# GpSimd's bias additions in two halves: cross-attention and a factored feed-forward layer on one core

## The chip, the core and the metric

The kernel runs on one core of a Trainium2 chip. The core has engines that run side by side, each with its own instruction queue: TensorE (PE, matmuls; its weight loads are listed apart as PEld), VectorE (DVE), ScalarE (ACT), GpSimd (POOL) and SyncE (SP, which here issues most of the DMAs). They meet through semaphores. The on-chip memory is SBUF; matmul results land in PSUM. The metric is the device time of one execution in microseconds (us), as the median of a few runs.

## The reference

The input x has 8 batches of 1024 rows of 1024 float32 numbers. What is computed:

```python
def _layernorm(x, axis=-1, eps=1e-05):
    m = jnp.mean(x, axis=axis, keepdims=True)
    v = jnp.var(x, axis=axis, keepdims=True)
    return (x - m) / jnp.sqrt(v + eps)
...
def reference(x, ctx_2048, mask_BxS2_bk0, L0_ffn_factors, L0_ffn_bias):
    def _L0_xattn_ref(hidden_states, memory_tokens, memory_mask):
        ...
        scores = jnp.einsum('bsd,bmd->bsm', hidden_states, memory_tokens) * scale
        scores = jnp.where(memory_mask[:, None, :], scores, neg_inf)
        attn = jax.nn.softmax(scores, axis=-1)
        readout = jnp.einsum('bsm,bmd->bsd', attn, memory_tokens)
        ...
    def _L0_ffn_ref(x, factors, bias):
        ...
        mixed = jnp.einsum('btd,rde->bte', x, factors)
        mixed = mixed / math.sqrt(rank) + bias
        return mixed
    x = x + _L0_xattn_ref(_layernorm(x, axis=-1), ctx_2048, mask_BxS2_bk0)
    x = x + _L0_ffn_ref(_layernorm(x, axis=-1), L0_ffn_factors, L0_ffn_bias)
    return x
```

The memory has 64 tokens in each batch, and there are 8 factors of 1024x1024. So each row attends to 64 tokens, the readout is added to it, the sum is normalized, multiplied by the sum of the factors, scaled, and added back together with the bias.

## The kernel before

The 8192 rows are worked in 16 groups of 512 rows. A group holds four row tiles of 128x1024 in SBUF, the tiles x. A tile is found by two numbers, h and q, as tile 2h+q. The steps of a group are: load the rows (load_rows, and once more in another layout, load_blocks); transpose them on VectorE (transpose_blocks, line 356, two instructions of 128x256 a call); scores on TensorE (line 399) with softmax (lines 426 to 439: line 426 reads PSUM, line 431 adds the mask in SBUF); the readout (line 465) and its addition to x (residual, line 473); the statistics and the normalization (normalize, line 534, ScalarE, which reads the tile x and writes h); a DMA that turns h into another layout (relayout), and VectorE's transposes of it (line 560); then the product with the summed factors.

That product is done by Strassen's scheme: seven products of half-size blocks, three of which (2, 3 and 4) are again split in seven. The operands' sums are formed by VectorE in combine_rows (lines 573 to 582, 128x512) and combine_parts (lines 621 to 631, 128x256): each of these instructions reads two SBUF tiles. TensorE multiplies in product (line 592) and part (line 641). VectorE adds each result, scaled, to x in give (line 605, 128x512) and give_part (line 655, 128x256): these read PSUM and the tile x.

The bias is added to x as a separate step, add_bias (line 540), between the normalization of a tile and the last addition of its products. It runs on GpSimd, on a whole tile of 128x1024, and reads two SBUF tiles, x and the broadcast bias. One tile of the first group has it on VectorE (add_bias_v, line 544). GpSimd has little else: small instructions on 128x2 numbers for the means and the reciprocal deviations (lines 317 to 346 and 490 to 520), on the way to the normalization.

The order is written out by hand. Two tables of step names, START and LOOP, are run line by line under a manual schedule; each engine takes its instructions in this order. START prepares the factors (their sum, and the combined blocks for the split products, combine_factors, lines 728 to 731) together with the first group and parts of the next. LOOP is run once for each group g, with p the group before it, n the next and m the one after that. In one pass it adds the bias of the tiles 3 and 1 of g and of the tiles 0 and 2 of n. PSUM banks and SBUF tiles are handed out from lists of free ones.

Of the kernel before, what the change touches and what calls it, by code (L numbers as in the profile page):

```python
# [10 lines left out]
F32 = mybir.dt.float32  # L11
BF16 = mybir.dt.bfloat16
AF = mybir.ActivationFunctionType
ALU = mybir.AluOpType
# [20 lines left out]
normalize 0 0 1; load_factor 1 7; load_factor 2 3; load_factor 2 5; load_factor 1 4;  # L35
transpose_h_pe 0 0 0; sum_factor 2 7; add_factor 1 7; load_factor 1 3; transpose_x_pe 1 0;
load_factor 1 6; add_sums 0 0; transpose_h_pe 0 0 1; read_out 0 1 0; add_factor 2 3;
add_bias 0 0 1; sum_factor 2 5; load_rows 1 3; load_factor 1 1; residual 0 1 0; norm_stats 0 1 0;
sum_factor 1 4; sum_factor 1 1; load_factor 2 1; load_rows 1 2; combine_rows 0 0 1;
sum_factor 2 1; norm_stats 0 1 1; add_factor 1 3; load_factor 2 2; add_factor 1 6;  # L40
load_factor 2 0; add_sums 1 1; row_sums 1 0; load_factor 3 0; add_sums 1 0; transpose_x_pe 1 1;
add_factor 2 2; add_factor 2 0; add_bias_v 0 0 0; add_sums 2 1; row_squares 1 0; load_factor 3 4;
add_factor 3 4; scores 1; add_factor 3 0; add_sums 2 0; product 0 0 1; load_factor 3 2;
normalize 0 1 0; normalize 0 1 1; transpose_h_pe 0 1 0; load_factor 3 3; add_factor 3 3;
row_sums 1 1; load_factor 3 1; load_factor 3 6; combine_rows 0 0 2; load_factor 3 7;
transpose_h_pe 0 1 1; product 0 0 5; row_squares 1 1; combine_rows 0 0 3; load_factor 3 5;
add_factor 3 2; sum_factor 3 1; combine_rows 0 0 4; scores_back 1; sum_factor 3 6; give 0 0 1;
load_rows 2 1; load_rows 2 0; add_factor 3 7; combine_rows 0 1 1; sum_factor 3 5; softmax 1;
add_sums 3 1; row_sums 2 0; product 0 1 1; weights_back 1; product 0 0 6; add_sums 3 0;
read_out 1 0 0; combine_parts 0 4 1; combine_factors 4; residual 1 0 0; read_out 1 0 1;  # L50
combine_rows 0 1 2; part 0 4 2; give 0 0 6; part 0 4 1; give_part 0 4 1; combine_parts 0 4 2;
combine_rows 0 1 3; part 0 4 5; residual 1 0 1; load_blocks 2 1; load_blocks 2 0;
combine_rows 0 1 4; product 0 0 7; give 0 1 1; norm_stats 1 0 0; row_squares 2 0;
give_part 0 4 2; combine_parts 0 4 3; read_out 1 1 0; add_bias 0 1 0; norm_stats 1 0 1;
product 0 1 6; part 0 4 6; combine_parts 0 2 1; load_rows 2 2; residual 1 1 0; read_out 1 1 1;
combine_parts 0 4 4; give_part 0 4 6; give 0 1 6; residual 1 1 1; product 0 1 5; normalize 1 0 0;
product 0 1 7; give_part 0 4 5; combine_factors 3; normalize 1 0 1; load_memory 2;
combine_factors 2; part 0 4 7; give 0 0 5; give_part 0 4 7; give 0 0 7; part 0 4 3; part 0 2 1;
transpose_blocks 2 0 0; part 0 2 5; norm_sums 1 1; centre_memory 2; transpose_blocks 2 0 1;
give_part 0 4 3; combine_parts 0 2 2; give_part 0 2 1; transpose_blocks 2 0 2; part 0 4 4;  # L60
combine_parts 0 3 1; transpose_memory 2; relayout 1 0; give_part 0 4 4; part 0 3 1; part 0 3 2;
add_bias 1 0 0; transpose_blocks 2 1 0; store 0 2; part 0 2 6; give_part 0 3 2; part 0 3 5;
transpose_blocks 2 1 1; give_part 0 2 5; norm_squares 1 1; transpose_blocks 2 0 3;
transpose_blocks 2 1 2; part 0 2 2; normalize 1 1 0; combine_parts 0 2 3; transpose_blocks 2 1 3;
normalize 1 1 1; give_part 0 2 6; combine_parts 0 2 4; combine_parts 0 3 2; transpose_rows 1 0 0;
# [2 lines left out]
product 1 0 1; give_part 0 3 5; scores_back 2; relayout 1 1; part 0 3 6; combine_rows 1 0 2;  # L68
give_part 0 2 7; give_part 0 3 6; product 1 0 5; combine_parts 0 3 4; give 0 1 7; part 0 3 3;
part 0 3 7; softmax 2; give_part 0 2 3; give 1 0 1; combine_rows 1 0 3; part 0 2 4;  # L70
transpose_rows 1 1 0; product 1 0 6; give_part 0 3 7; add_bias 0 1 1; weights_back 2; part 0 3 4;
store 0 3; give_part 0 2 4; read_out 2 0 0; read_out 2 0 1; add_bias 1 0 1; transpose_rows 1 1 1;
add_bias 1 1 0; give 1 0 6; give_part 0 3 4; product 1 1 1;
"""

LOOP = """
# [1 line left out]
product g 0 6; give p 1 5; transpose_rows g 1 0; give_part p 3 4; give g 0 5; give_part p 2 3;  # L78
give g 0 6; weights_back n; transpose_rows g 1 1; part p 3 3; read_out n 0 0; give_part p 3 2;
combine_rows g 1 1; read_out n 0 1; residual n 0 0; residual n 0 1; give_part p 3 3;  # L80
product g 1 1; combine_parts g 4 1; product g 0 7; load_blocks m 1; add_bias g 1 1;
combine_rows g 0 4; read_out n 1 0; norm_stats n 0 0; combine_rows g 1 2; read_out n 1 1;
norm_stats n 0 1; transpose_blocks m 0 0; part g 4 5; end_rows p 1; end_rows p 0; part g 4 1;
residual n 1 0; product g 1 5; store p 3; combine_rows g 1 3; combine_parts g 4 2;
give_part g 4 1; part g 4 6; combine_rows g 1 4; give g 1 1; product g 1 6; normalize n 0 0;
combine_parts g 2 1; normalize n 0 1; add_bias n 0 0; store p 1; transpose_blocks m 0 1;
give_part g 4 5; part g 2 5; combine_parts g 4 3; load_memory m; give_part g 4 6;
combine_parts g 4 4; residual n 1 1; combine_parts g 2 2; store p 0; part g 2 1; give g 0 7;
part g 4 7; give g 1 6; combine_parts g 3 1; norm_sums n 1; part g 4 2; centre_memory m;
part g 3 1; part g 4 3; combine_parts g 2 3; give_part g 4 7; give_part g 4 2; add_bias g 1 0;  # L90
give_part g 2 1; transpose_memory m; transpose_blocks m 0 2; norm_squares n 1;
combine_parts g 2 4; part g 4 4; give_part g 3 1; give_part g 2 5; give_part g 4 4;
transpose_blocks m 0 3; part g 2 6; give_part g 2 6; add_bias n 0 1; give_part g 4 3;
combine_parts g 3 2; part g 3 5; relayout n 0; product g 1 7; load_rows m 0; normalize n 1 0;
transpose_blocks m 1 0; transpose_blocks m 1 1; part g 3 6; combine_parts g 3 3; store g 2;
normalize n 1 1; part g 2 7; transpose_rows n 0 0; give g 1 7; load_rows m 2;
combine_parts g 3 4; give_part g 3 6; give_part g 2 7; transpose_rows n 0 1; load_rows m 1;
part g 2 2; load_rows m 3; transpose_blocks m 1 2; row_sums m 0; row_sums m 1;
transpose_blocks m 1 3; scores m; product n 0 1; scores_back m; combine_rows n 0 1; part g 3 7;
combine_rows n 0 2; row_squares m 0; give_part g 2 2; combine_rows n 0 3; give_part g 3 5;  # L100
part g 2 4; give_part g 3 7; product n 0 5; part g 3 4; relayout n 1;
# [4 lines left out]
def kernel(  # L106
# [17 lines left out]
    nc = tc.nc  # L124
    P = 128
# [7 lines left out]
    KH = NC // 2  # L133
    NS = NC // 2
    H = D // 2
    HH = H // 2
# [3 lines left out]
    ISR = 1.0 / math.sqrt(R)  # L140
# [8 lines left out]
    work = ctx.enter_context(tc.tile_pool(name="work", bufs=1))  # L149
# [3 lines left out]
    class Slots:  # L153
# [28 lines left out]
    bias_bc = const.tile([P, D], F32, name="bias_bc")  # L182
# [9 lines left out]
    SECOND = (2, 3, 4)  # L192
    PRODUCTS = {
        1: ("a11", "b11", "u", True, ((0, 0),)),
        5: ("s1", "t1", "v", True, ((1, 1), (0, 1)) if 3 in SECOND else ((1, 1),)),
        6: ("s2", "t2", "u", False, ((0, 1),)),
        3: ("s4", "b22", "v", False, ((0, 1),)),
        7: ("s3", "t3", "u", False, ((1, 1), (1, 0)) if 4 in SECOND else ((1, 1),)),
        2: ("a12", "b21", "z", True, ((0, 0),)),
        4: ("a22", "t4", "u", False, ((1, 0),)),  # L200
    }
    LAST = {"u": 7 if 4 in SECOND else 4, "v": 5 if 3 in SECOND else 3, "z": 2}
    PARTS = {
        1: ("a11", "u", True, (0, 0)),
        5: ("s1", "v", True, (1, 1)),
# [18 lines left out]
    st = {}  # L224
# [310 lines left out]
                to, fr, AF.Identity, bias=nb[:, h : h + 1], scale=rstd[:, h : h + 1]  # L535
            )

    def add_bias(g: int, q: int, h: int):
        xt = st["x", g, 2 * h + q]
        nc.gpsimd.tensor_add(xt, xt, bias_bc)  # L540

    def add_bias_v(g: int, q: int, h: int):
        xt = st["x", g, 2 * h + q]
        nc.vector.tensor_add(xt, xt, bias_bc)

    def relayout(g: int, q: int):
        h2 = st["h", g, q]
# [19 lines left out]
    def combine_rows(g: int, q: int, k: int):  # L567


        ops = st["ops", g, q]  # L570
        if k == 1:
            ops["s1"] = work.tile([P, KH, P], F32, tag="s1", name=f"s1_{g}_{q}")
            nc.vector.tensor_add(ops["s1"], ops["a21"], ops["a22"])
        if k == 2:
            ops["s2"] = work.tile([P, KH, P], F32, tag="s2", name=f"s2_{g}_{q}")
            nc.vector.tensor_sub(ops["s2"], ops["s1"], ops["a11"])
        if k == 3:
            nc.vector.tensor_sub(ops["a21"], ops["a11"], ops["a21"])
            ops["s3"] = ops["a21"]
        if k == 4:  # L580
            assert "s3" in ops
            nc.vector.tensor_sub(ops["a11"], ops["a12"], ops["s2"])
            ops["s4"] = ops["a11"]
# [17 lines left out]
    def give(g: int, q: int, p: int):  # L601
        key = PRODUCTS[p][2]
        for h, n in PRODUCTS[p][4]:
            xt = st["x", g, 2 * h + q][:, ts(n, H)]
            nc.vector.scalar_tensor_tensor(xt, st["y", g, q, key], ISR, xt, ALU.mult, ALU.add)  # L605
        if LAST[key] == p:
            banks.back(("y", g, q, key))
# [41 lines left out]

    def give_part(g: int, p: int, i: int):  # L650
        key = PARTS[i][1]
        h, n = PRODUCTS[p][4][0]
        q, k = PARTS[i][3]
        xt = st["x", g, 2 * h + q][:, 2 * n * HH + k * HH : 2 * n * HH + (k + 1) * HH]
        nc.vector.scalar_tensor_tensor(  # L655
            xt, st["yp", g, p, key][:, :HH], ISR, xt, ALU.mult, ALU.add
        )
        if LAST2[key] == i:
            banks.back(("yp", g, p, key))

# [125 lines left out]
```

## Time and profile before

| what | us |
|---|---|
| median of three runs | 981.09 (979.46 to 981.38) |
| the profiled execution | 981.39 |
| its span, first to last instruction | 979.6 |
| GpSimd's bias additions, 63 of 128x1024 | 150.1, mean 2.384 |
| VectorE line 627, 48 of 128x256, two SBUF inputs | 45.9, mean 0.957 |
| VectorE line 625, 48 of the same form | 20.9, mean 0.434 |
| VectorE line 582, 32 of 128x512, two SBUF inputs | 41.9, mean 1.308 |
| VectorE line 576, 32 of the same form | 21.4, mean 0.668 |
| VectorE line 431, 16 of 128x256, two SBUF inputs | 30.7, mean 1.916 |
| TensorE busy, 256 to 312 us | 55.04 of 56 |
| VectorE busy, 256 to 312 us | 50.20 of 56 |

The granted TensorE clock is 0.996 of full speed over the span. A profile of one execution gives each instruction's start and length. A group of instructions is one line, engine, operation and set of tiles; beside its busy time stands the idle time of its engine just before it, and what ended that. A chain of waits is followed back from a late instruction: at each step to what released it, or to the instruction before it on its engine. The last groups of the input differ from the steady loop, as do the first 200 us, in which the factors are loaded and summed.

### The profile page before, as it was taken

Reading aid. Unit: us, or ns where it says so; the run is one execution under the profiler, and the core shown is the slowest. Engines: PE = TensorE matmul, PEld = TensorE weight load, DVE = VectorE, ACT = ScalarE, POOL = GpSimd, SP = SyncE. Lnnn points to the kernel's source line nnn. Section 1 sums busy time; section 2 is a strip of 40 time slices with the busy share of each in tenths; the row PEclk is TensorE's granted clock in tenths of the full one; section 3 lists DMA queues with packets and bytes.
Section 4 is the critical chain, followed back from the end, with each engine's and each line's share of the span. In section 5 each row is a group of like instructions: output and inputs, shape, how many; then the busy total and the mean of one; then the engine's idle time right before and its main releaser. Section 6 shows DMA issues by size and latency. Waiting matters only on the chain.

```text
span 979.6 us, 11017 instructions
## 1 busy us (share of the span) xinstructions
PE 941.1 (96%) x3456; PEld 547.0 (56%) x3456; DVE 838.6 (86%) x1510; ACT 380.8 (39%) x712; POOL 237.9 (24%) x298
## 2 busy tenths in 40 slices
PE   3889999999999999999999999999999999999998
PEld 2345455655656565655656565564656565565656
DVE  3689999979799887989799697989889788989955
ACT  3035252443616253442623455351714445252300
POOL 0021124312312232411322142321223123132300
PEclk9999999999999999999999999999999999999999
DMA  9999637475565667366465756557474746542412
GB/s 353 418 421 369 179 107 159 126 177 145 158 156 155 151 194 149 109 168 165 153 162 155 164 144 148 140 162 176 151 177 134 172 123 170 142 151 79 100 70 86
DMA packets 93530, 167.01 MB, mean 170 GB/s; under 512 B 12320, under 2 KB 71840, under 8 KB 89376
## 3 DMA queue, kind: packets, MB, share of 16 engines
q1 hardware_dynamic: 93024, 165.20, 58.4%
q10 hardware_dynamic: 448, 1.11, 0.4%
q8 instruction: 27, 0.44, 0.2%
q14 instruction: 31, 0.25, 0.1%
HBM read 101.25 MB, written 33.55 MB: 138 GB/s over the span
## 4 chain that ended last, share of the span: by engine, by line
PE 60%; DVE 26%; DMA 5%; SPq 4%; issue 3%; ACT 1%; POOL 0%; DVEq 0%; ACTq 0%; POOLq 0%
PE yu L592 24%; PE yv L592 7%; PE ro L465 5%; PE y4u L641 4%; SPq L551 4%; PE y3u L641 4%; DVE xT L356 4%; DVE x L655 3%; DVE x L605 3%; DVE hT L560 3%; PE scT L399 3%; DMA f<-in_L_ffn_factors_dram 3%; DVE hT L627 3%; PE y2u L641 2%; PE y4v L641 2%
## 5 line engine op out<-in xcount | busy, mean ns | idle before, releaser
L534 ACT ACTIVATE h<-x,nb,rstd 128x512 f32<-128x512 f32 x128 | 96.2, 822 | 211.6 <-DVE x L473 134.2
L540 POOL TENSOR_TENSOR x<-x,bias_bc 128x1024 f32<-128x1024 f32 x63 | 150.1, 2384 | 73.5 <-DVE x L605 37.7
L592 PE MATMUL yu<-b,hT 128*128 128x512 f32 x256 | 118.0, 604 | 0.0
L592 PE MATMUL yu<-t,s 128*128 128x512 f32 x256 | 115.3, 593 | 0.1
L592 PE MATMUL yv<-t,s 128*128 128x512 f32 x256 | 115.2, 593 | 0.0
L592 PE MATMUL yu<-t,hT 128*128 128x512 f32 x256 | 115.1, 592 | 0.0
L605 DVE SCALAR_TENSOR_TENSOR x<-yu,x 128x512 f32<-128x512 f32 x128 | 82.9, 675 | 19.1 <-PE yu L592 19.1
L473 DVE SCALAR_TENSOR_TENSOR x<-ro,rden,x 128x512 f32<-128x512 f32 x128 | 88.4, 741 | 3.5 <-PE ro L465 3.5
L316 ACT ACTIVATE junk<-x 128x1024 bf16<-128x1024 f32 x60 | 63.2, 1054 | 56.6 <-DMA x<-in_x_dram 55.7
L356 DVE STREAM_TRANSPOSE xT<-xb 128x256 f32<-128x256 f32 x224 | 81.6, 410 | 0.0
L592 PEld LDWEIGHTS yu<-b,hT 128*128 128x128 f32 x256 | 46.3, 189 | 62.6 <-issue 51.8
L592 PEld LDWEIGHTS yu<-t,hT 128*128 128x128 f32 x256 | 48.6, 190 | 54.4 <-issue 50.5
L592 PEld LDWEIGHTS yu<-t,s 128*128 128x128 f32 x256 | 48.4, 190 | 48.7 <-issue 45.7
L592 PEld LDWEIGHTS yv<-t,s 128*128 128x128 f32 x256 | 48.5, 190 | 48.2 <-issue 45.9
L399 PE MATMUL scT<-xT,memT 128*64 128x256 f32 x512 | 66.5, 385 | 9.2 <-DVE xT L356 9.2
L560 DVE STREAM_TRANSPOSE hT<-hb 128x1024 f32<-128x1024 f32 x60 | 73.5, 1227 | 0.7 <-issue 0.6
L328 ACT ACTIVATE junk<-x,nmean 128x1024 bf16<-128x1024 f32 x60 | 68.9, 1149 | 2.9 <-POOL nmean L317 0.7
L490 POOL TENSOR_SCALAR rstd<-mv 128x2 f32<-128x2 f32 x17 | 4.6, 269 | 253.6 <-DVE mv L487 253.6
L465 PE MATMUL ro<-mem,eT 64*128 64x512 f32 x256 | 64.5, 617 | 0.6 <-ACT eT L454 0.6
L655 DVE SCALAR_TENSOR_TENSOR x<-y3u,x 128x256 f32<-128x256 f32 x64 | 26.2, 409 | 43.9 <-PE y3u L641 43.6
L502 ACT ACTIVATE junkz<-x 128x1024 bf16<-128x1024 f32 x30 | 31.7, 1056 | 72.7 <-DVE x L473 72.2
L399 PEld LDWEIGHTS scT<-xT,memT 128*64 128x64 f32 x512 | 37.3, 136 | 36.0 <-DVE xT L356 15.0
(133 smaller groups left out, 1544.2 us busy)
## 6 DMA issues: line engine op xcount, KB each, us to landing
f<-in_L_ffn_factors_dram SPq DMA_DIRECT2D x32, 1024.0 KB, 10.8
x<-in_x_dram SPq DMA_DIRECT2D x64, 512.0 KB, 4.5
out_dram<-x SPq DMA_DIRECT2D x64, 512.0 KB, 4.4
hb<-h SPq DMA_DIRECT2D x480, 64.0 KB, 2.0
xb<-in_x_dram SPq DMA_DIRECT2D x112, 256.0 KB, 6.9
mem<-in_ctx_dram SPq DMA_DIRECT2D x14, 256.0 KB, 3.8
mem<-in_ctx_dram ACTq DMA_DIRECT2D x2, 256.0 KB, 5.8
bias_bc<-in_L_ffn_bias_dram ACTq DMA_DIRECT2D x1, 512.0 KB, 7.9
```

The source lines that it names most:

```text
L316: nc.scalar.activation(junk, st["x", g, t], AF.Copy, accum_out=s1[:, t : t + 1])
L328: nc.scalar.activation(junk, st["x", g, t], AF.Square, bias=nmean[:, t : t + 1], accum_out=ss[:, t : t + 1])
L356: nc.vector.transpose(xT[:, 2 * e + c].rearrange("p (t j) -> p t j", j=Q), xb.rearrange("p t (k e i c) -> p e c t k i", e=NC // 2, i=2, c= ...
L399: nc.tensor.matmul(ps[ts(h, M), : 2 * P], mT[:, c, :], st["xT", g, h][:, c, :], start=(c == 0), stop=(c == NC - 1),)
L465: nc.tensor.matmul(ps, eT[ts(h, M), q, :], m[ts(h, M), ts(n, H)], start=True, stop=True)
L473: nc.vector.scalar_tensor_tensor(xt, st.pop(("ro", g, q, n, h)), rden[:, k : k + 1], xt, ALU.mult, ALU.add)
L534: nc.scalar.activation(to, fr, AF.Identity, bias=nb[:, h : h + 1], scale=rstd[:, h : h + 1])
L540: nc.gpsimd.tensor_add(xt, xt, bias_bc)
L560: nc.vector.transpose(st["hT", g, q][:, h].rearrange("p c (t j) -> p t c j", j=Q), hb[:, h].rearrange("p t (c i) -> p t c i", i=Q),)
L592: nc.tensor.matmul(ps, lhs[:, c, :], wq[right][:, c, :], start=(first and c == 0), stop=(c == KH - 1), skip_group_check=True,)
L605: nc.vector.scalar_tensor_tensor(xt, st["y", g, q, key], ISR, xt, ALU.mult, ALU.add)
L641: nc.tensor.matmul(ps, lhs[:, c, :], wp[p][i][:, c, :], start=(first and c == 0), stop=(c == 1), skip_group_check=True,)
```

## The change

Each call of add_bias now names a half tile: its last number k runs from 0 to 3, where k // 2 is the old h and k % 2 the half of 512 columns. In the tables each old entry is replaced by two, one behind the other at the same place. add_bias_v does the same on VectorE. So GpSimd has 126 additions of 128x512 in place of 63 of 128x1024, and VectorE two in place of one.

```diff
-add_bias 0 0 1; sum_factor 2 5; load_rows 1 3; load_factor 1 1; residual 0 1 0; norm_stats 0 1 0;
...
+add_bias 0 0 2; add_bias 0 0 3; sum_factor 2 5; load_rows 1 3; load_factor 1 1; residual 0 1 0;
...
-product g 1 1; combine_parts g 4 1; product g 0 7; load_blocks m 1; add_bias g 1 1;
...
+product g 1 1; combine_parts g 4 1; product g 0 7; load_blocks m 1; add_bias g 1 2;
+add_bias g 1 3; combine_rows g 0 4; read_out n 1 0; norm_stats n 0 0; combine_rows g 1 2;
...
-        6: ("s2", "t2", "u", False, ((0, 1),)),
+        6: ("s2", "t2", "u", False, ((0, 1), (1, 1), (1, 0)) if 7 in SECOND else ((0, 1),)),
...
-    LAST = {"u": 7 if 4 in SECOND else 4, "v": 5 if 3 in SECOND else 3, "z": 2}
+    LAST = {"u": 6 if 7 in SECOND else 7 if 4 in SECOND else 4, "v": 5 if 3 in SECOND else 3, "z": 2}
...
-    def add_bias(g: int, q: int, h: int):
-        xt = st["x", g, 2 * h + q]
-        nc.gpsimd.tensor_add(xt, xt, bias_bc)
-
-    def add_bias_v(g: int, q: int, h: int):
-        xt = st["x", g, 2 * h + q]
-        nc.vector.tensor_add(xt, xt, bias_bc)
+    def add_bias(g: int, q: int, k: int, eng=nc.gpsimd):
+
+        xt = st["x", g, 2 * (k // 2) + q][:, ts(k % 2, H)]
+        eng.tensor_add(xt, xt, bias_bc[:, ts(k % 2, H)])
+
+    def add_bias_v(g: int, q: int, k: int):
+        add_bias(g, q, k, nc.vector)
...
-            ops["s1"] = work.tile([P, KH, P], F32, tag="s1", name=f"s1_{g}_{q}")
+            ops["s1"] = work.tile([P, KH, P], F32, tag=f"s1{q if 5 in SECOND else ''}", name=f"s1_{g}_{q}")
...
-        h, n = PRODUCTS[p][4][0]
         q, k = PARTS[i][3]
-        xt = st["x", g, 2 * h + q][:, 2 * n * HH + k * HH : 2 * n * HH + (k + 1) * HH]
-        nc.vector.scalar_tensor_tensor(
-            xt, st["yp", g, p, key][:, :HH], ISR, xt, ALU.mult, ALU.add
-        )
+        for h, n in PRODUCTS[p][4]:
+            xt = st["x", g, 2 * h + q][:, ts(2 * n + k, HH)]
+            nc.vector.scalar_tensor_tensor(
+                xt, st["yp", g, p, key][:, :HH], ISR, xt, ALU.mult, ALU.add
+            )
```

SECOND is (2, 3, 4), at line 192, in both kernels.

More of the change, by code (lines that the diff above doesn't have):

```diff
@@ L37 @@
 load_factor 1 6; add_sums 0 0; transpose_h_pe 0 0 1; read_out 0 1 0; add_factor 2 3;
-add_bias 0 0 1; sum_factor 2 5; load_rows 1 3; load_factor 1 1; residual 0 1 0; norm_stats 0 1 0;
[L39 to L60, printed above, removed]
@@ L61 @@
-combine_parts 0 3 1; transpose_memory 2; relayout 1 0; give_part 0 4 4; part 0 3 1; part 0 3 2;
-add_bias 1 0 0; transpose_blocks 2 1 0; store 0 2; part 0 2 6; give_part 0 3 2; part 0 3 5;
+add_bias 0 0 2; add_bias 0 0 3; sum_factor 2 5; load_rows 1 3; load_factor 1 1; residual 0 1 0;
+norm_stats 0 1 0; sum_factor 1 4; sum_factor 1 1; load_factor 2 1; load_rows 1 2;
+combine_rows 0 0 1; sum_factor 2 1; norm_stats 0 1 1; add_factor 1 3; load_factor 2 2;
+add_factor 1 6; load_factor 2 0; add_sums 1 1; row_sums 1 0; load_factor 3 0; add_sums 1 0;
@@ new lines @@
+transpose_x_pe 1 1; add_factor 2 2; add_factor 2 0; add_bias_v 0 0 0; add_bias_v 0 0 1;
+add_sums 2 1; row_squares 1 0; load_factor 3 4; add_factor 3 4; scores 1; add_factor 3 0;
+add_sums 2 0; product 0 0 1; load_factor 3 2; normalize 0 1 0; normalize 0 1 1;
+transpose_h_pe 0 1 0; load_factor 3 3; add_factor 3 3; row_sums 1 1; load_factor 3 1;
+load_factor 3 6; combine_rows 0 0 2; load_factor 3 7; transpose_h_pe 0 1 1; product 0 0 5;
+row_squares 1 1; combine_rows 0 0 3; load_factor 3 5; add_factor 3 2; sum_factor 3 1;
@@ new lines @@
+combine_rows 0 0 4; scores_back 1; sum_factor 3 6; give 0 0 1; load_rows 2 1; load_rows 2 0;
+add_factor 3 7; combine_rows 0 1 1; sum_factor 3 5; softmax 1; add_sums 3 1; row_sums 2 0;
+product 0 1 1; weights_back 1; product 0 0 6; add_sums 3 0; read_out 1 0 0; combine_parts 0 4 1;
+combine_factors 4; residual 1 0 0; read_out 1 0 1; combine_rows 0 1 2; part 0 4 2; give 0 0 6;
+part 0 4 1; give_part 0 4 1; combine_parts 0 4 2; combine_rows 0 1 3; part 0 4 5; residual 1 0 1;
+load_blocks 2 1; load_blocks 2 0; combine_rows 0 1 4; product 0 0 7; give 0 1 1;
@@ new lines @@
+norm_stats 1 0 0; row_squares 2 0; give_part 0 4 2; combine_parts 0 4 3; read_out 1 1 0;
+add_bias 0 1 0; add_bias 0 1 1; norm_stats 1 0 1; product 0 1 6; part 0 4 6; combine_parts 0 2 1;
+load_rows 2 2; residual 1 1 0; read_out 1 1 1; combine_parts 0 4 4; give_part 0 4 6; give 0 1 6;
+residual 1 1 1; product 0 1 5; normalize 1 0 0; product 0 1 7; give_part 0 4 5;
+combine_factors 3; normalize 1 0 1; load_memory 2; combine_factors 2; part 0 4 7; give 0 0 5;
+give_part 0 4 7; give 0 0 7; part 0 4 3; part 0 2 1; transpose_blocks 2 0 0; part 0 2 5;
@@ L63 @@
+norm_sums 1 1; centre_memory 2; transpose_blocks 2 0 1; give_part 0 4 3; combine_parts 0 2 2;
+give_part 0 2 1; transpose_blocks 2 0 2; part 0 4 4; combine_parts 0 3 1; transpose_memory 2;
+relayout 1 0; give_part 0 4 4; part 0 3 1; part 0 3 2; add_bias 1 0 0; add_bias 1 0 1;
+transpose_blocks 2 1 0; store 0 2; part 0 2 6; give_part 0 3 2; part 0 3 5;
 transpose_blocks 2 1 1; give_part 0 2 5; norm_squares 1 1; transpose_blocks 2 0 3;
@@ L70 @@
 part 0 3 7; softmax 2; give_part 0 2 3; give 1 0 1; combine_rows 1 0 3; part 0 2 4;
-transpose_rows 1 1 0; product 1 0 6; give_part 0 3 7; add_bias 0 1 1; weights_back 2; part 0 3 4;
-store 0 3; give_part 0 2 4; read_out 2 0 0; read_out 2 0 1; add_bias 1 0 1; transpose_rows 1 1 1;
-add_bias 1 1 0; give 1 0 6; give_part 0 3 4; product 1 1 1;
+transpose_rows 1 1 0; product 1 0 6; give_part 0 3 7; add_bias 0 1 2; add_bias 0 1 3;
+weights_back 2; part 0 3 4; store 0 3; give_part 0 2 4; read_out 2 0 0; read_out 2 0 1;
+add_bias 1 0 2; add_bias 1 0 3; transpose_rows 1 1 1; add_bias 1 1 0; add_bias 1 1 1; give 1 0 6;
+give_part 0 3 4; product 1 1 1;
 """
@@ L80 @@
 combine_rows g 1 1; read_out n 0 1; residual n 0 0; residual n 0 1; give_part p 3 3;
-product g 1 1; combine_parts g 4 1; product g 0 7; load_blocks m 1; add_bias g 1 1;
-combine_rows g 0 4; read_out n 1 0; norm_stats n 0 0; combine_rows g 1 2; read_out n 1 1;
-norm_stats n 0 1; transpose_blocks m 0 0; part g 4 5; end_rows p 1; end_rows p 0; part g 4 1;
-residual n 1 0; product g 1 5; store p 3; combine_rows g 1 3; combine_parts g 4 2;
+product g 1 1; combine_parts g 4 1; product g 0 7; load_blocks m 1; add_bias g 1 2;
@@ L85 @@
+add_bias g 1 3; combine_rows g 0 4; read_out n 1 0; norm_stats n 0 0; combine_rows g 1 2;
+read_out n 1 1; norm_stats n 0 1; transpose_blocks m 0 0; part g 4 5; end_rows p 1; end_rows p 0;
+part g 4 1; residual n 1 0; product g 1 5; store p 3; combine_rows g 1 3; combine_parts g 4 2;
 give_part g 4 1; part g 4 6; combine_rows g 1 4; give g 1 1; product g 1 6; normalize n 0 0;
-combine_parts g 2 1; normalize n 0 1; add_bias n 0 0; store p 1; transpose_blocks m 0 1;
-give_part g 4 5; part g 2 5; combine_parts g 4 3; load_memory m; give_part g 4 6;
@@ L88 @@
[L88 to L98, printed above, removed]
+combine_parts g 2 1; normalize n 0 1; add_bias n 0 0; add_bias n 0 1; store p 1;
@@ new lines @@
+transpose_blocks m 0 1; give_part g 4 5; part g 2 5; combine_parts g 4 3; load_memory m;
+give_part g 4 6; combine_parts g 4 4; residual n 1 1; combine_parts g 2 2; store p 0; part g 2 1;
+give g 0 7; part g 4 7; give g 1 6; combine_parts g 3 1; norm_sums n 1; part g 4 2;
+centre_memory m; part g 3 1; part g 4 3; combine_parts g 2 3; give_part g 4 7; give_part g 4 2;
+add_bias g 1 0; add_bias g 1 1; give_part g 2 1; transpose_memory m; transpose_blocks m 0 2;
+norm_squares n 1; combine_parts g 2 4; part g 4 4; give_part g 3 1; give_part g 2 5;
@@ new lines @@
+give_part g 4 4; transpose_blocks m 0 3; part g 2 6; give_part g 2 6; add_bias n 0 2;
+add_bias n 0 3; give_part g 4 3; combine_parts g 3 2; part g 3 5; relayout n 0; product g 1 7;
+load_rows m 0; normalize n 1 0; transpose_blocks m 1 0; transpose_blocks m 1 1; part g 3 6;
+combine_parts g 3 3; store g 2; normalize n 1 1; part g 2 7; transpose_rows n 0 0; give g 1 7;
+load_rows m 2; combine_parts g 3 4; give_part g 3 6; give_part g 2 7; transpose_rows n 0 1;
+load_rows m 1; part g 2 2; load_rows m 3; transpose_blocks m 1 2; row_sums m 0; row_sums m 1;
```

## The prediction

> **What bounds the kernel now.** I read the page's busy times first, then the waits, then TensorE's timeline where it waits, then the chain backwards from there.
>
> ```profile
> PE 941.1 (96%) x3456; PEld 547.0 (56%) x3456; DVE 838.6 (86%) x1510; ACT 380.8 (39%) x712; POOL 237.9 (24%) x298
> ```
>
> TensorE (PE) bounds it; VectorE (DVE) is a close second; GpSimd (POOL), whose instructions change, is three quarters idle. So POOL's own time can't matter; whom it holds up can. The waits of PE between 200 and 872 us, the steady loop:
>
> ```profile
> PE scT L399 <- DVE xT L356: 8.4, 11, 0.8
> PE sc L417 <- ACT scTs L407: 0.5, 1, 0.5
> ```
>
> The loop has one recurring wait: the scores matmuls wait for VectorE's block transposes, once in each group (the whole trace has 12). PE ends are modelled, so I price it from starts. The timeline of PE at a scores block without the wait, then at one with it (start, length, both us):
>
> ```profile
> 199.05 3.67 PE L399 MATMUL scT<-xT,memT 128*64 128x256 f32 x32
> 202.65 0.70 PE L592 MATMUL yu<-b,hT 128*128 128x512 f32 x1
> ...
> 253.96 2.37 PE L399 MATMUL scT<-xT,memT 128*64 128x256 f32 x18
> 257.06 1.94 PE L399 MATMUL scT<-xT,memT 128*64 128x256 f32 x14 [0.73 <-DVE xT L356]
> 258.93 0.70 PE L592 MATMUL yu<-b,hT 128*128 128x512 f32 x1
> ```
>
> From the first scores matmul to the product behind it is 3.60 us undisturbed and 4.97 with the wait: 1.37 us lost. In the other parity of groups (309.40 to 314.44) it is 5.04, so 1.44. Twelve such waits, six of each parity, are 6 x 1.37 + 6 x 1.44 = **16.9 us**, all that can be won in the loop. Why are the transposes late? The chain of waits up to 257.06:
>
> ```profile
> 246.31 0.42 DVE x L655
> ...
> 249.72 2.49 DVE hT L627
> 252.20 1.16 DVE hT L560
> ...
> 257.06 1.94 PE scT L399 x14
> ```
>
> From 246.31, where VectorE last waited for PE, it works without a gap, and one instruction of it, L627, takes 2.5 us. The groups by line (min/median/max in ns) say what that should take:
>
> ```profile
> L627 DVE TENSOR_TENSOR hT<-hT,hT x48: 375/410/2584, 121.0 to 964.5; 128x256 f32<-128x256 f32 x48
> L582 DVE TENSOR_TENSOR hT<-hT,s x32: 681/686/2674, 98.4 to 949.2; 128x512 f32<-128x512 f32 x32
> L631 DVE TENSOR_TENSOR hT<-hT,r x48: 382/404/2533, 125.1 to 969.0; 128x256 f32<-128x256 f32 x48
> L431 DVE TENSOR_TENSOR sm<-sm,maskf x16: 424/2114/2342, 28.8 to 881.9; 128x256 f32<-128x256 f32 x16
> ```
>
> All four read two SBUF tiles. The stretched ones lie under a bias addition:
>
> ```profile
> 249.56 2.37 POOL L540 TENSOR_TENSOR x<-x,bias_bc 128x1024 f32<-128x1024 f32 x1
> 249.64 2.56 DVE L627 TENSOR_TENSOR hT<-hT,hT 128x256 f32<-128x256 f32 x1
> ```
>
> L627 ends at 252.20, 0.27 after the addition's end at 251.93. VectorE's operations with one SBUF input (L655 and L605 read PSUM and x; the transposes) keep their length under the same additions. The Trainium skill has this rule ("SBUF — State Buffer", Who interferes with whom): a VectorE instruction with two SBUF inputs and a GpSimd instruction that reads SBUF exclude each other for a whole instruction. The trace agrees, at about 2.2 us a hit.
>
> **The change, part by part.** *Work added.* 63 additions of 128x1024 become 126 of 128x512. The row of 128x1024 has 2.36 us (its median); the nearest row with hardly any elements, POOL's TENSOR_TENSOR at L493 (128x2), has 0.215. That gives (2.36 - 0.215) / 1022 = 2.1 ns an element and 0.215 + 510 x 0.0021 = 1.29 us for a half. Bounds: 1.18 (no fixed part) to 1.34 (fixed part 0.31, the dearest small row, L317). So POOL gains some 0.2 us x 63 = 14 us of work in 740 us of idle time. It would show only where POOL has something queued behind: L517 behind the addition at 296.95 starts at 299.51, 0.1 after that ends. It slips by some 0.4 us; it feeds a normalization whose rows are transposed only in the next pass of the loop. I cost it at nothing; without that cover it is 0.4 us in six groups, 2.4.
>
> *Start table.* VectorE's one bias addition (L544, 1.22 us) becomes two; two 128x512 additions in a row at L714 take 1.27. Plus 0.05, on VectorE's chain.
>
> *The other edits* of the diff (the products' table, one tile's tag, the loop in give_part) choose, with SECOND = (2, 3, 4) and one target for each split product, what was chosen before: nothing.
>
> *What moves.* A VectorE instruction held by the first half gets in when that half ends, 1.29 us after its start instead of 2.36: **1.07 us earlier** (1.02 to 1.18), if the lock comes free between the halves. That is the one unknown. The rule of the same section speaks against it: issue order decides who waits. Both halves are issued back to back, so strictly the second, queued before L627 comes, goes first, and L627 waits for both. But the trace has four whole additions in a row:
>
> ```profile
> 155.92 2.35 POOL L540 TENSOR_TENSOR x<-x,bias_bc 128x1024 f32<-128x1024 f32 x1 [1.49 <-DVE x L605]
> 158.23 2.54 POOL L540 TENSOR_TENSOR x<-x,bias_bc 128x1024 f32<-128x1024 f32 x1
> 160.72 2.81 POOL L540 TENSOR_TENSOR x<-x,bias_bc 128x1024 f32<-128x1024 f32 x1
> 163.49 2.36 POOL L540 TENSOR_TENSOR x<-x,bias_bc 128x1024 f32<-128x1024 f32 x1
> ...
> 156.21 2.34 DVE L431 TENSOR_TENSOR sm<-sm,maskf 128x256 f32<-128x256 f32 x1
> 159.85 1.46 DVE L578 TENSOR_TENSOR hT<-hT 128x512 f32<-128x512 f32 x1
> ```
>
> L431 ends at 158.55, 0.28 after the first addition, and the second lasts 0.19 longer than usual; L578 ends at 161.31, 0.54 after the second, and the third is 0.45 longer. VectorE was let in between twice, though POOL's next instruction had started. By the row I win 1.07 us a hit; by the rule each costs about 0.15 more. I take the row.
>
> *Sum, even groups* (257 us kind). VectorE's last wait for PE is at 246.31; then only L627 collides. Behind it stand L560 (a transpose) and two L605 (PSUM), so the second half runs beside them. 1.07 of the 1.37 us is won; the transposes are then some 0.3 late instead. 6 x 1.07 = 6.4.
>
> *Odd groups* (312 us kind). Three hits on the way: L582 at 288.32, L627 at 297.12, L631 at 301.31. After L582 comes L605, then L621 with two inputs, which meets the second half: about half a microsecond is left. Of that and of L627's 1.07, the waits for fresh PSUM results at L655 (y4u, y4z, whose matmuls start at 297.24 and 298.10) take back a part. L631 is followed by three L655 and two transposes: 1.07 kept. So between 1.07 and all 1.44; I take 1.3, as some of the earlier gain survives. 6 x 1.3 = 7.8.
>
> *Places that win nothing.* The softmax hit (L431) is followed by VectorE waits for PE (1.17 us idle before 274.07), which swallow it. In the start table, L730 at 132.09 is followed by L731, two inputs again: the stall moves to the second half; and L627 at 120.99 begins in what will be the second half and ends 0.17 later. Against it, the wait of PE's weight load at 159.99 (0.52 us, for an L605 behind the first stall) should shrink. Net 0. Behind 872 us PE does not wait: nothing. What is late next is the same transposes, in even groups.
>
> Total -(6.4 + 7.8) = -14.2 us. The profiled execution took 981.39 (span 979.6 and 1.8 around it): 967.2. The median of the three runs, 981.09, is 0.3 under it. I say **967.2 us**.
>
> **The rivals.**
> - *VectorE is not let in.* In favour: the rule above; these halves write one tile with nothing between them. Then a hit lasts 2 x 1.29 - 0.04 (starts overlap so) = 2.54 instead of 2.36, 0.18 more: even groups 6 x 0.18, odd ones up to three hits, 6 x 0.36: 3.2 us, **984.6**, slower. It decides at the lock between halves alone. Against: the four in a row. 0.06.
> - *The stall only moves to the second half.* For: L730/L731 and L582/L621 do that. Against: L627 and L631, which count, have one-input work behind them for 2 us. Then 981.4, no change (a measurement here can't tell 0.2%, 2 us, from none). 0.06.
> - *Half is won*: one parity gains, or another release (POOL's delayed chain, 2.4 us; a DMA) takes the place of the transposes: 981.4 - 7 = **974**. For: VectorE had been late, so other slack was never tested. 0.16.
> - *All is won*: the odd groups fully and the even ones too, because VectorE comes 0.3 earlier than worked out: 981.4 - 16.9 = 964.5. 0.12.
> - The forecast itself: 0.60.
>
> **Range.** 964 to 975.5 holds the forecast with its bounds (1.02 to 1.18 us a hit in even groups, 1.07 to 1.44 in odd ones: 12.5 to 15.7 us won), the half case and the full one. Faster by over 0.2%: 0.60 + 0.16 + 0.12 = 0.88; within 0.06; slower 0.06.
>
> **What would show it.** Right: L431, L627, L582, L631 at most about 1.6 us long; their sum over the usual length, now some 83 us (16 x 1.49 + 48 x 0.55 + 32 x 0.62 + 48 x 0.26), about halved; scores blocks of 3.6 to 3.9 us; some second halves 0.2 to 0.5 longer than the first. Wrong: stretched operations of 2.5 us that span both halves; new stretched rows, L621 or L625, in place of the old; scores blocks still of 5 us. If the hits are halved and the time is not, the transposes were not what PE waited for.

## The result, and the profile after

The changed kernel takes 965.37 us (median of 4 runs, 964.01 to 966.25); the kernel before, on the same chip, 981.16. The ratio is 0.984, with a 95% interval of 0.982 to 0.986. The profiled execution took 964.01 us, with a span of 962.2. TensorE's granted clock was 1.00 of full speed in it, against 0.996 in the profile before: there it was halved (0.50) for about 3 us near 48 and near 72 us, in the start. A repeat of the changed kernel, further below, has two such dips as well and scores blocks of the same length, so the clock does not make the difference in the loop.

The page of the changed kernel, busy times and the shares of the chain that ended last. Lines of the kernel behind the tables have moved by two or three: L629, L584, L633, L433 and L623 are now what was L627, L582, L631, L431 and L621.

```profile
PE 931.7 (97%) x3456; PEld 546.7 (57%) x3456; DVE 801.4 (83%) x1511; ACT 380.8 (40%) x712; POOL 259.5 (27%) x361
...
PE 87%; DMA 5%; DVE 5%; issue 1%; SPq 1%; ACT 0%; DVEq 0%; ACTq 0%
```

VectorE is busy 37.2 us less, GpSimd 21.6 more. VectorE had 26% of the chain before and has 5% now: it rarely comes last. In the list of waits, PE has none between 200 and 860 us. The scores blocks on PE's timeline, one of each parity of groups:

```profile
252.56 3.95 PE L401 MATMUL scT<-xT,memT 128*64 128x256 f32 x32
256.44 0.70 PE L594 MATMUL yu<-b,hT 128*128 128x512 f32 x1
...
306.90 3.67 PE L401 MATMUL scT<-xT,memT 128*64 128x256 f32 x32
310.51 0.70 PE L594 MATMUL yu<-b,hT 128*128 128x512 f32 x1
```

Read from start to start: 3.88 us in even groups (4.97 before) and 3.60 or 3.61 in odd ones (5.04 before). The even ones still lose 0.28, in pauses too short for the list of waits. The twelve blocks together take 44.93 us instead of 60.15: **15.2 us**. The rest of the 17.4 us between the two profiled spans is not the change's: 1.4 lie ahead of the first of these blocks, and a repeat of the changed kernel had 0.5 more there than the kernel before; 0.8 is a single stretch near 540 us, where the kernel before has its one wait for ScalarE (L407, in the prediction's list), whose work had waited for a load of x. It comes and goes whatever the additions are: the profile with tiles 0 and 2 halved has it as well, the one with the additions whole and one entry moved has not (both below).

The collision in an even group, GpSimd's two halves and VectorE beside them:

```profile
248.16 1.27 POOL L543 TENSOR_TENSOR x<-x,bias_bc 128x512 f32<-128x512 f32 x1
249.38 1.47 POOL L543 TENSOR_TENSOR x<-x,bias_bc 128x512 f32<-128x512 f32 x1
...
248.24 1.47 DVE L629 TENSOR_TENSOR hT<-hT,hT 128x256 f32<-128x256 f32 x1
249.63 1.23 DVE L562 STREAM_TRANSPOSE hT<-hb 128x1024 f32<-128x1024 f32 x1
```

L629 ends at 249.71, 0.28 after the first half's end at 249.43; under the whole addition it had ended at 252.20, 0.27 after. The second half is 0.2 us longer than the first: it had started, but L629 came to its end first. The transpose L562 then runs at its usual length beside it. By line, min/median/max in ns:

```profile
L629 DVE TENSOR_TENSOR hT<-hT,hT x48: 378/418/1491, 119.7 to 947.1; 128x256 f32<-128x256 f32 x48
L584 DVE TENSOR_TENSOR hT<-hT,s x32: 679/688/1115, 96.6 to 931.8; 128x512 f32<-128x512 f32 x32
L633 DVE TENSOR_TENSOR hT<-hT,r x48: 381/414/1300, 123.9 to 951.6; 128x256 f32<-128x256 f32 x48
L433 DVE TENSOR_TENSOR sm<-sm,maskf x16: 424/1030/1256, 28.1 to 864.5; 128x256 f32<-128x256 f32 x16
L623 DVE TENSOR_TENSOR r<-hT x48: 371/426/1452, 108.7 to 940.0; 128x256 f32<-128x256 f32 x48
```

Where the longest were 2.3 to 2.7 us, they are 1.1 to 1.5. L623 was stretched in 3 of its 48 instances before (as L621), and is in 22 now: part of the stall has moved to it.

In one place VectorE was not let in between the halves. It lies in the start, in the combined factors:

```profile
130.95 3.09 DVE L732 TENSOR_TENSOR tau<-b 128x512 f32<-128x512 f32 x1
...
131.00 1.27 POOL L543 TENSOR_TENSOR x<-x,bias_bc 128x512 f32<-128x512 f32 x1
...
132.23 1.26 POOL L543 TENSOR_TENSOR x<-x,bias_bc 128x512 f32<-128x512 f32 x1
```

L732, which takes 0.69 undisturbed, starts 0.05 us ahead of the first half, and still ends 0.55 behind the second; neither half is longer than usual. From 110 us on, an instruction with two SBUF inputs was held at an addition with the next one right behind it 50 times in this profile, and 49 times it was done before that next one. The exception returns at this instruction in every profile below in which this addition is cut by columns, in quarters too (3.34 us over four pieces). What sets it apart, other than its start just ahead of the first piece, stays open. It costs 0.12 us against the whole addition (2.97), once.

### The profile page after: what moved, and what is told of

It is laid out like the page before. It is cut to its first block, busy times and chain, and to the rows that moved or that the text cites. A ratio compares the mean times of both kernels' runs of the same rounds, so it can differ in the third digit from the quotient of the medians.

```text
span 962.2 us, 11083 instructions
## 1 busy us (share of the span) xinstructions
PE 931.7 (97%) x3456; PEld 546.7 (57%) x3456; DVE 801.4 (83%) x1511; ACT 380.8 (40%) x712; POOL 259.5 (27%) x361
## 4 chain that ended last, share of the span: by engine, by line
PE 87%; DMA 5%; DVE 5%; issue 1%; SPq 1%; ACT 0%; DVEq 0%; ACTq 0%
PE yu L594 33%; PE yv L594 11%; PE scT L401 6%; PE y3u L643 6%; PE y2u L643 6%; PE y4u L643 6%; PE ro L467 6%; DMA f<-in_L_ffn_factors_dram 4%; PE y4v L643 3%; PE y3v L643 3%; PE y2v L643 3%; PE y3z L643 1%; PE y2z L643 1%; PE y4z L643 1%; DMA x<-in_x_dram 1%; DVE b L691 1%
## 5 line engine op out<-in xcount | busy, mean ns | idle before, releaser
L543 POOL TENSOR_TENSOR x<-x,bias_bc 128x512 f32<-128x512 f32 x126 | 170.9, 1377 | 70.4 <-DVE x L607 35.8
L562 DVE STREAM_TRANSPOSE hT<-hb 128x1024 f32<-128x1024 f32 x60 | 73.6, 1228 | 3.1 <-DMA hb<-h 2.9
L401 PE MATMUL scT<-xT,memT 128*64 128x256 f32 x512 | 60.5, 383 | 0.0
L706 PE MATMUL sum<-f,ident 128*128 128x512 f32 x96 | 43.7, 601 | 7.3 <-DMA f<-in_L_ffn_factors_dram 7.1
```

What stands on the lines that cost most here:

```text
L401: nc.tensor.matmul(ps[ts(h, M), : 2 * P], mT[:, c, :], st["xT", g, h][:, c, :], start=(c == 0), stop=(c == NC - 1),)
L543: eng.tensor_add(xt, xt, bias_bc[:, ts(k % 2, H)])
L562: nc.vector.transpose(st["hT", g, q][:, h].rearrange("p c (t j) -> p t c j", j=Q), hb[:, h].rearrange("p t (c i) -> p t c i", i=Q),)
```

## The experiments

Unless a text says otherwise, each kernel is the one before with GpSimd's additions changed as its diff shows. Of each timed kernel the text gives the median, and the ratio to the runs of the kernel before on the same chip with its interval. Blocks are the twelve scores blocks, even groups first. What the two engines exclude each other from is called "the port" or "the lock" in the expectations.

**Only the addition before the scores halved.** CUTS gives the column cuts by tile.

```diff
+    CUTS = {0: (0, 1024), 1: (0, 1024), 2: (0, 512, 1024), 3: (0, 1024)}
...
-        nc.gpsimd.tensor_add(xt, xt, bias_bc)
+        cuts = CUTS[2 * h + q]
+        for a, b in zip(cuts, cuts[1:]):
+            nc.gpsimd.tensor_add(xt[:, a:b], xt[:, a:b], bias_bc[:, a:b])
```

> Only the bias addition of tile 2 (the last before the scores) is halved; tiles 0, 1 and 3 keep the whole addition. Theory (the port is let go between halves, and only a hit without a later wait for fresh matmul results counts): even groups' scores blocks 3.88 us as with all halved; odd groups gain 1.09 of 1.44 from this hit alone, so about 3.95; together 6 x 1.09 + 6 x 1.1 = 13 us under the kernel before, near 968. Rival (each of the four additions adds its share): a quarter of the gain, some 4 us.

Measured: 967.06 us, ratio 0.987 (0.984 to 0.990); blocks of 3.88 and 3.94, together 13.2 us less than before.

**The other three halved, this one whole.** The loop over the cuts stays in every run with CUTS; from here on the diff shows the cuts alone.

```diff
+    CUTS = {0: (0, 512, 1024), 1: (0, 512, 1024), 2: (0, 1024), 3: (0, 512, 1024)}
```

> The other part: tiles 0, 1 and 3 halved, tile 2 whole. Theory: even groups' scores blocks stay at 4.97; odd ones keep the 0.35 us won before, so 4.7; 2 us under the kernel before, near 979. Rival (each its share): three quarters of the gain, some 11 us.

Measured: 979.35 us, ratio 0.9982 (0.9975 to 0.9990); blocks of 4.97 and 4.69, together 2.2 us less. So 13 of the 15 us hang on 16 of the 63 additions, and the shares are far from equal. A hit can also be new: the block at 197.6 us, ahead of these twelve, takes 4.53 us instead of 3.60. Tile 2's addition comes 0.9 us earlier there, measured from the block, and now covers L635 (L631 before), which takes 2.40 us instead of 0.38.

**Halves for tiles 0 and 2 alone.**

```diff
+    CUTS = {0: (0, 512, 1024), 1: (0, 1024), 2: (0, 512, 1024), 3: (0, 1024)}
```

> Tiles 0 and 2 halved, tiles 1 and 3 whole. Theory (in odd groups the hit on L582 behind tile 0's addition gives 0.35 us, the one before the scores 1.09, tile 1's nothing): 3.88 and 3.60 us, as fast as all halved. Rival (tile 1's or tile 3's share is needed): odd blocks 3.9.

Measured: 965.75 us, ratio 0.986 (0.984 to 0.987); blocks of 3.88 and 3.60, as with all halved. Tiles 1 and 3 add nothing.

**No bias on GpSimd.**

The result lacks the bias in all tiles but one.

```diff
-        nc.gpsimd.tensor_add(xt, xt, bias_bc)
+        pass
```

> GpSimd's bias additions are left out (the bias is missing from all tiles but one). Theory: the additions cost the kernel nothing but their hold on VectorE's second read; all scores blocks 3.60 us, 6 x 1.37 + 6 x 1.44 = 16.9 us under the kernel before, near 964 at the same clock, and VectorE busy some 85 us less than before (838.6). Rival (TensorE waits for something else as well): scores blocks still over 3.6.

Measured: 962.52 us, ratio 0.982 (0.980 to 0.984); all blocks 3.60, together 16.9 us less; VectorE busy 752.1, 86.5 less than before. That is the whole price of the additions in the loop, and PE's list of waits is empty there: nothing else is late behind them.

**The first piece shorter, or longer.** Tile 2's addition is cut in 256 and 768 columns, then in 768 and 256; the others are halved.

```diff
+    CUTS = {0: (0, 512, 1024), 1: (0, 512, 1024), 2: (0, 256, 1024), 3: (0, 512, 1024)}
...
+    CUTS = {0: (0, 512, 1024), 1: (0, 512, 1024), 2: (0, 768, 1024), 3: (0, 512, 1024)}
```

> As all halved, but tile 2's addition is cut in 256 and 768 columns. Theory: the held instruction gets in after about 0.2 + 254 x 0.0021 = 0.75 us, 1.6 earlier than under a whole addition, more than the 1.37 us an even group lacks: even and odd blocks both 3.60, 16.9 us under the kernel before, 1.7 under all halved; the long second piece lies beside one-input work. Rival (the number of pieces counts, not the first one's length): 3.88 as with halves.

> As all halved, but tile 2's addition is cut in 768 and 256 columns. Theory: the first piece lasts 0.2 + 766 x 0.0021 = 1.8 us, so only 0.55 us is won at this hit: even scores blocks 4.4, odd 5.04 - 0.35 - 0.55 = 4.15; 6 x 0.55 + 6 x 0.9 = 8.7 us under the kernel before. Rival (the number of pieces counts): 3.88 and 3.60 as with halves.

Measured: 963.33 us, ratio 0.982 (0.980 to 0.984), with all blocks 3.60; and 972.10, ratio 0.991 (0.990 to 0.993), with blocks of 4.43 and 4.14. An even block with the short piece first, then one with the long piece first:

```profile
253.15 3.67 PE L399 MATMUL scT<-xT,memT 128*64 128x256 f32 x32
256.75 0.70 PE L596 MATMUL yu<-b,hT 128*128 128x512 f32 x1
```
```profile
254.99 2.37 PE L399 MATMUL scT<-xT,memT 128*64 128x256 f32 x18
257.55 1.94 PE L399 MATMUL scT<-xT,memT 128*64 128x256 f32 x14 [0.18 <-DVE xT L356]
259.42 1.12 PE L596 MATMUL yu<-b,hT 128*128 128x512 f32 x2
```

The count of pieces is two each time; the block follows the first one's length: 3.60, 3.88, 4.43 and 4.97 us in even groups for 256, 512, 768 and 1024 columns. The steps of 0.55 and 0.54 are 256 columns at 2.1 ns; the last, 0.28, is cut off where the wait is gone.

**All in quarters.**

```diff
+    CUTS = {0: (0, 256, 512, 768, 1024), 1: (0, 256, 512, 768, 1024), 2: (0, 256, 512, 768, 1024), 3: (0, 256, 512, 768, 1024)}
```

> All additions cut in four of 128x256. Theory: the first piece holds 0.75 us, so the first instruction is let in 1.6 us earlier; even and odd blocks 3.60; 16.9 us under the kernel before, if the later pieces do not hold up two-input work again; POOL busy about 4 x 0.75 x 63 = 190 us of additions. Rival (more pieces, more holds): VectorE busy above that of halves (801 us) and blocks over 3.6.

Measured: 964.01 us, ratio 0.983 (0.982 to 0.985); all blocks 3.60; VectorE busy 777.3, less than with halves; GpSimd busy 284.7 against 259.5. The later pieces hold nobody up for long.

**Cut by partitions instead of columns.**

```diff
-        nc.gpsimd.tensor_add(xt, xt, bias_bc)
+        for r in range(2):
+            rows_ = slice(64 * r, 64 * r + 64)
+            nc.gpsimd.tensor_add(xt[rows_], xt[rows_], bias_bc[rows_])
```

> All additions cut in two by partitions, 64x1024 each, one behind the other. Theory (what counts is how long one piece holds the port, and a piece takes as long as it has columns): each piece lasts 2.3 us, the held instruction still waits 2.2 us, and a second hold of 2.3 us follows: even blocks 5.0 us as before, odd ones 5 to 6.5 since L621 behind L582 now meets a second full piece; the kernel before or up to 10 us slower. Rival (two instructions, or half the data each, is what helps): as fast as the column halves.

Measured: 1024.8 us, ratio 1.046 (1.044 to 1.049); blocks of 6.26 to 7.96, where I had written 5.0 and 5 to 6.5. That pieces of half the rows do not help is as the theory says, the size is not: 43 us where I had written up to 10. This kernel's additions by line, an even group's collisions (here L627 is r<-r,hT, L625 before, and L629 is hT<-hT,hT), and the waits of PE and one of VectorE from 200 to 920 us:

```profile
L542 POOL TENSOR_TENSOR x<-x,bias_bc x126: 2335/2422/3222, 53.1 to 1001.5; 64x1024 f32<-64x1024 f32 x126
```
```profile
256.58 4.88 POOL L542 TENSOR_TENSOR x<-x,bias_bc 64x1024 f32<-64x1024 f32 x2
...
256.91 2.31 DVE L627 TENSOR_TENSOR r<-r,hT 128x256 f32<-128x256 f32 x1
...
260.49 1.25 DVE L629 TENSOR_TENSOR hT<-hT,hT 128x256 f32<-128x256 f32 x1
```
```profile
PE scT L399 <- DVE xT L356: 25.2, 12, 2.2
PE y3u L643 <- DVE r L627: 6.4, 7, 1.0
PE y4u L643 <- DVE x L657: 4.3, 5, 0.9
...
DVE x L657 <- POOL x L542: 13.4, 7, 1.9
```

A piece of half the rows takes as long as the whole, so a whole addition now takes 4.9 us. Its two pieces catch two VectorE instructions in an even group, not one as I had reckoned. VectorE also waits for the sums themselves, which it did not in the loop before: the step that adds a product to x stands until the slower addition to x is done, up to 1.9 us. And PE waits for two more things. How the 43 us divide between the longer holds and this later result no run separates. The 43.2 us between the spans are 18.1 in the scores blocks, 13.9 in the stretches between them, 8.1 ahead of the first and 3.1 behind the last.

**GpSimd writes, but does not read.** The bias is left out of the result here.

```diff
-        nc.gpsimd.tensor_add(xt, xt, bias_bc)
+        for _ in range(2):
+            nc.gpsimd.memset(bias_bc, 0.0)
```

> Each addition on GpSimd is replaced by two fills of a 128x1024 tile with zeros, which read nothing (the bias is left out of the result). Theory[...]: no VectorE instruction is stretched although GpSimd writes about 0.95 us a fill at the same places; L627, L582, L631 and L431 keep 0.4 and 0.68 us, scores blocks 3.60, as without the bias. Rival (any GpSimd work on SBUF holds VectorE): stretches of about 1 to 2 us remain.

Measured: 961.37 us, ratio 0.981 (0.979 to 0.983); all blocks 3.60. Two fills lie where the addition lay, and L627 starts 0.11 us behind the first:

```profile
247.41 1.96 POOL L540 MEMSET bias_bc<- 128x1024 f32 x2
...
247.52 0.39 DVE L627 TENSOR_TENSOR hT<-hT,hT 128x256 f32<-128x256 f32 x1
```
```profile
L431 DVE TENSOR_TENSOR sm<-sm,maskf x16: 424/424/427, 28.4 to 862.7; 128x256 f32<-128x256 f32 x16
```

L431 has one length, 424 to 427 ns. GpSimd is busy 206 us and holds nobody. So it is not GpSimd's writing to SBUF that holds VectorE; what the additions have beyond the fills is that they read, and this fits the rule that the prediction cites. A GpSimd instruction that reads one tile only was not run.

**The collision taken away with the additions whole.** One entry of LOOP is moved; the additions are as before.

```diff
-transpose_blocks m 1 0; transpose_blocks m 1 1; part g 3 6; combine_parts g 3 3; store g 2;
+transpose_blocks m 1 0; transpose_blocks m 1 1; part g 3 6; store g 2;
...
-combine_parts g 3 4; give_part g 3 6; give_part g 2 7; transpose_rows n 0 1; load_rows m 1;
+combine_parts g 3 3; combine_parts g 3 4; give_part g 3 6; give_part g 2 7; transpose_rows n 0 1; load_rows m 1;
```

> All additions whole, as before; one entry of LOOP is moved: combine_parts g 3 3 (L627) goes behind transpose_rows n 0 0 and give g 1 7, so that in even groups a transpose and two readers of PSUM, 2.5 us of work, lie beside tile 2's addition. Theory (only the collision costs): even blocks 3.60, odd ones 5.04 as before, where L631 is hit: 6 x 1.37 = 8.2 us under the kernel before. Rival (the addition's length itself, or its place, delays the transposes): even blocks stay near 5.

Measured: 974.22 us, ratio 0.994 (0.993 to 0.995); even blocks 3.67, odd ones 5.17 (one 5.39), together 6.9 us less, of 8.2 forecast. With the additions whole, the even groups' loss is gone but for 0.07: it was the place of L627 beside the addition. The odd groups, hit elsewhere, gain nothing and lose over 0.1, which I did not follow up.

**Is the short first piece better than halves?** Both again, with more executions on one chip.

> The changed kernel again, on the same chip as the next runs, with more rounds: 0.984 of the time before, scores blocks 3.88 and 3.60 us.

> Tile 2 cut in 256 and 768 columns, the others in halves, again with more rounds: even blocks 3.60 instead of 3.88, so 6 x 0.28 = 1.7 us under the changed kernel. Rival: the two do not differ.

Measured: 964.54 us (ratio 0.9845, 0.9831 to 0.9858) and 963.94 (0.9834, 0.9820 to 0.9847). The blocks differ as expected, 3.88 against 3.60 in six groups, 1.7 us in the traces; the times differ by 0.6, and their intervals overlap. The start, before the first of these blocks, scatters by 2.5 us (252.0 and 254.5 us in these two profiles), which hides it. What makes the start scatter stays open. It is not the granted clock alone: the start of 252.0 has 0.50 of full speed from 45.2 to 51.5 us, the later one of the changed kernel above, 252.6, has full speed.

## Why the prediction was right

*What bounds the kernel*: TensorE, losing up to 16.9 us in twelve scores blocks. The run without the additions gained 16.9 us in those blocks, and PE's list of waits is empty in the loop of the changed kernel.

*A half lasts 1.29 us*: 1.278 by the median. *A held instruction comes in 1.07 us earlier*: 1.47 instead of 2.56 for L627, 1.09.

*The unknown, whether the lock comes free between the halves*: decided with the row of four additions, against the strict reading of issue order. The second half's 1.47 us after the first one's 1.27 shows VectorE let in, as do 49 of the 50 hits. The rival in which it is not let in (984.6 us) is seen once, at L732 in the start, and in no hit before the scores blocks of the loop. Its price a hit, put at 0.15 in one place and 0.18 in another, is 0.18 by the working shown (2.54 - 2.36).

*Even groups, 1.07 of 1.37 us won and 0.3 left*: 1.09 won, 0.28 left. The cuts at 256 and 768 columns confirm the slope.

*Odd groups, between 1.07 and all 1.44, taken as 1.3*: all 1.44, so 0.8 us more in six groups. Here the size came near by a wrong path in one place, which is luck. I had the gain at L627 survive in part. Instead GpSimd's addition moved against VectorE. Before, L621 started 0.16 us ahead of it and was not held:

```profile
296.95 2.47 POOL L540 TENSOR_TENSOR x<-x,bias_bc 128x1024 f32<-128x1024 f32 x1
...
296.79 0.41 DVE L621 TENSOR_TENSOR r<-hT 128x256 f32<-128x256 f32 x1
```

Now, measured from the scores block behind them, the addition comes 0.6 us earlier and this instruction (L623) 0.2, so that it meets the first half, and L627 (L629) the second:

```profile
293.88 1.27 POOL L543 TENSOR_TENSOR x<-x,bias_bc 128x512 f32<-128x512 f32 x1
295.12 1.45 POOL L543 TENSOR_TENSOR x<-x,bias_bc 128x512 f32<-128x512 f32 x1
```
```profile
294.08 1.36 DVE L623 TENSOR_TENSOR r<-hT 128x256 f32<-128x256 f32 x1
295.36 1.49 DVE L629 TENSOR_TENSOR hT<-hT,hT 128x256 f32<-128x256 f32 x1
```

Together they take 2.85 us where the same two had taken 2.99: this is the rival of the stall that only moves, in one place, and L621 is the new stretched row that the prediction names as a sign of being wrong. It did not decide, because the hit on L631 behind it gave its 1.1 back in full. The odd groups' gain is L582's 0.35 and L631's 1.1, as the runs with tile 2 alone (3.94 us blocks), without tile 2 (4.69) and with tiles 0 and 2 (3.60) show by parts.

*Places that win nothing*: the softmax hit (tile 3) and tile 1 add nothing, by the run with tiles 0 and 2 alone. In the start, the cost of L730 was right and the path wrong: the stall did not move on to L731 (0.68 us, as before); L730 itself, L732 in the changed kernel, was held over both halves.

*The stretched time about halved*: VectorE's busy time fell by 37.2 us of the 86.5 that the run without the additions gives back.

*GpSimd's added work, hidden*: forecast 14 us, found 20.8 in its additions (170.9 against 150.1), since a half that lets VectorE in is longer, by 0.2 us for 128x256. No wait of PE came of it.

*The sum*: 14.2 us forecast, 15.2 found in the blocks; what the median shows beyond that (15.8) lies within the scatter of the start.

## What to carry to other kernels

Look for instructions of one engine whose length varies by a factor of several, and see what runs on the other engine beside the long ones; here a GpSimd busy for 24% of the span cost TensorE 16.9 us. A long GpSimd instruction that reads SBUF can be cut along its columns (not its rows) so that a two-input VectorE instruction behind it gets in sooner. It then waits for the first piece only, and the rest costs nothing if what follows on VectorE has one SBUF input for as long as it lasts. Look at the trace afterwards: one instruction here, at 131 us, was not let in at all, and an addition that comes earlier can hit an instruction that it had missed. The cut is worth only what the engine that waits in the end can gain: 16 of the 63 additions held 13 of the 15 us.

## What the runs showed of the hardware that was not expected

The exclusion passes from one instruction to the next, though GpSimd's next one has started: a VectorE instruction of 128x256 between two pieces lengthened the second by 0.2 us (1.47 against 1.27) and ended 0.28 us behind the first. The prediction had only two such places to go by; the changed kernel has 49. Not expected was the fiftieth case, where a VectorE instruction that had started 0.05 us ahead of two halves waited for both, and in another run for four quarters.

The length of an addition did not depend on its rows between 64 and 128: the shortest took 2.34 us in both cases (medians 2.42 and 2.36). The columns cost 2.1 ns each. That two pieces by rows would cost 43 us, by catching more instructions and by giving their result later, was not expected either.
